# Two lanes of filler work, a count of three PSUM banks, and one weight transform issued beside the next

## The chip, the core and the metric

The kernel runs on one core of one Trainium2 chip. Its engines work side by side and each takes its instructions in the order in which they were issued: TensorE (PE in the profile, its weight loads PEld) multiplies matrices into PSUM; VectorE (DVE) and ScalarE (ACT) work on SBUF and PSUM; GpSimd (POOL) works on SBUF here; SyncE (SP) issues the DMAs. The metric is the device time of one execution in microseconds (us), and of several runs the median.

## The reference

Two transformer layers over x of 2 x 1024 x 256, each of the form x + attention(norm(x)) + feed-forward(norm(x)).

- Layer 0: linear attention with elu(q) + 1 and elu(k) + 1 (16 heads of 16), and a gated feed-forward of 256 -> 1024 -> 256 with weights rounded to -1, 0, 1 times a scale.
- Layer 1: softmax attention with rotary positions, and a gated feed-forward whose input and hidden vectors go through a Walsh-Hadamard transform (`fwht`) and sign vectors first:

```python
x = fwht(x * SU_ug) / SCALE
x_up = x @ W_up.T * (Wscale_ug[:INTER] * SCALE)
x_gate = x @ W_gate.T * (Wscale_ug[INTER:] * SCALE)
x = jax.nn.silu(x_gate) * x_up
x = fwht(x * SU_dp) / SCALE
x = x @ W_down.T * (Wscale_dp * SCALE)
```

The kernel moves these transforms from the activations to the weights, which are transformed once.

## The kernel before

**Phases.** Everything up to about 200 us (norms, layer 0's attention, most of its feed-forward, the first heads and the first maxima) is put in order by a planner: `Plan.emit` sorts recorded operations by estimated costs and by the table `LEADS`. From there on the order is written out by the loops at the end of the kernel, and it is this part that the change touches.

**Units.** Layer 1's attention is cut into 8 units (2 batches x 4 groups of 4 heads). The main loop runs over units 0 to 6; each has 32 steps, and each step issues one burst on PE: the scores of the next unit for their maxima (`scm`) and the scores of this unit for the exponentials (`sce`). DVE reduces `scm` to `peak` (1.22 us), ACT turns `sce` into `pr` (1.02 us), and `weigh` multiplies `pr` with the values into `po` every fourth step. A unit takes some 88 us in the profile: unit 2 from about 390 us, unit 4 from about 566 us. Unit 7 has no maxima to find and ends near 880 us.

**Filler.** Between bursts, `slot` lets PE do other work. Generators yield after each group of matmuls, with the group's cost by the program's constants; `fill` steps the generator at the head of the list `filler` until the slot's share is spent. The share is what is left of all such work (`left`) over the slots that are left (`to_fill`). The filler is, in order: layer 0's last feed-forward pieces, `norm1(2)`, the weight transforms `hadamards()`, `norm1(3)`, and the eight pieces of layer 1's feed-forward, `ffn1(0)` to `ffn1(7)`. `project(b, n)`, the output projection of a quarter of the attention, is put at place 1 of the list when its attention is ready (`queue_next`).

**Waits.** A generator that yields SOON has issued matmuls whose result has still to be drained from PSUM. The drains are issued at the next `go_on(SOON, ...)`, once in two steps, or at once if `fill` still owes more than `LEAD` = 0.85. If less is owed, `fill` breaks off. FIRST and SECOND are such points too.

**Heads.** In units 0, 2 and 4 `heads_of` makes the next heads. It stands in the list `urgent`, which `stage` steps in every second step: there `lay_out` transposes four tiles into one bank `pt`, `take_out` drains it with an ACT cast to `qk_hi` and a DVE subtraction to `ql`, and the next row's projection `pqkv` goes into another bank.

**Banks.** [...] Two tiles "pair" hold the scores (4 banks), `po` holds one, and three are general, tag "bank": every `pug` (gate and up of one 128-wide block of the hidden layer), `py` (down), `pw` (weight transforms), `pt` (transposes) and `pqkv` takes one of them. A tile's place comes free when its last reader has finished; a matmul into a new tile waits for that on PE, and everything behind it in PE's order with it.

**The transforms.** `hadamard_down` multiplies layer 1's down weights by a 128-wide transform on PE; `butterflies` does the remaining three stages over the eight blocks with additions on POOL and subtractions on DVE, and then multiplies by signs on ACT. It runs in the list `background`, one yield for each `go_on`, between `wd1` (tag "wC") and a second buffer `other` (tag "wB"). `hadamard_in` transforms the gate weights (tag "wA") and the up weights, whose result also has the tag "wB". `hadamards` therefore waits, between these two, until the background is empty:

```python
yield from hadamard_in("wgT1", "wA")
while background:
    yield 0.0, SECOND
yield from hadamard_in("wuT1", "wB")
```

## Time and profile before

| | before |
|---|---|
| median of 3 runs | 895.97 us |
| lowest, highest | 893.58, 896.11 us |
| the profiled execution | 894.11 us |
| its span in the profile | 892.3 us |
| mean granted clock of TensorE | 0.994 |

In the page, busy time is given for each engine with its share of the span; slices are fortieths of the span (22.3 us each) with one digit for the busy tenths; PEclk is the clock granted to TensorE, where 9 stands for 90% or more. In the timeline a row has the start, the length, the engine, the operation, what it writes and reads, and in brackets the idle time of the engine before it and what ended that. A count such as x4 is the number of records merged into the row; an f32 matmul leaves two records. All instructions carry the line 316 because a helper issues them, so tiles are told apart by name.

### The profile page before, as it was taken

The page shows a single profiled execution, that of the slowest core. Times are in us where ns is not written, and L with a number is a line of the kernel's source. Part 1 is how long each engine was busy: PE and PEld are TensorE (multiplying, and loading weights), DVE is VectorE, ACT ScalarE, POOL GpSimd, SP SyncE. Part 2 cuts the span into 40 slices and gives each one's busy share as a digit, 9 for nine tenths or more (in the row PEclk, how much of TensorE's full clock was granted, in tenths as well). Part 3 has the DMA queues.
Part 4 walks back from the last instruction along what each step waited for, and adds up shares of the span by engine and source line. Part 5 has one row for each costly group of instructions (what it writes and reads, how often), then busy time and mean ns, then how long its engine had stood idle before and what let it go on. Part 6 is the DMA issues. An engine that isn't in the chain of part 4 may idle for free.

```text
span 892.3 us, 14588 instructions
## 1 busy us (share of the span) xinstructions
PE 851.7 (95%) x6048; PEld 509.3 (57%) x6048; DVE 578.0 (65%) x950; ACT 445.0 (50%) x657; POOL 209.9 (24%) x283
## 2 busy tenths in 40 slices
PE   8999999989989979999999999998999999999997
PEld 5699866675456534555555555554555555555533
DVE  5887567887767776657766656667665656656211
ACT  6645464515655454535544444454454444444563
POOL 2656877513551220104400000143000000000000
PEclk9999999999999989999999999999999999999999
DMA  9200000000010110000000000000100000000001
GB/s 303 84 1 1 1 1 1 1 1 1 1 49 1 48 47 1 2 1 1 1 1 1 1 2 1 1 1 13 36 1 1 1 1 1 1 2 1 1 7 42
DMA packets 11313, 14.77 MB, mean 17 GB/s; under 512 B 1264, under 2 KB 8944, under 8 KB 11248
## 3 DMA queue, kind: packets, MB, share of 16 engines
q1 hardware_dynamic: 11248, 13.85, 4.7%
q8 instruction: 47, 0.77, 0.4%
q14 instruction: 18, 0.15, 0.1%
HBM read 11.75 MB, written 2.10 MB: 16 GB/s over the span
## 4 chain that ended last, share of the span: by engine, by line
PE 80%; DVE 12%; ACT 4%; issue 2%; DMA 1%; SPq 0%; POOL 0%; ACTq 0%; DVEq 0%
PE pug L316 18%; PE scm L316 15%; PE py L316 13%; PE po L316 12%; PE sce L316 8%; DVE peak L316 6%; PE pqkv L316 5%; PE pt L316 4%; PE pkv L316 1%; ACT pr L316 1%; PE sc L316 1%; PE pq L316 1%; PE pw L316 1%; DVE act L316 1%; DVE att L316 1%
## 5 line engine op out<-in xcount | busy, mean ns | idle before, releaser
L316 ACT ACTIVATE pr<-sce 128x1024 f32<-128x1024 f32 x256 | 260.3, 1023 | 270.9 <-PE sce L316 270.7
L316 DVE TENSOR_REDUCE peak<-scm 128x2 f32<-128x1024 f32 x224 | 274.1, 1224 | 177.6 <-PE scm L316 175.7
L316 PE MATMUL sce<-qk_hi 32*128 32x512 f32 x512 | 124.3, 497 | 3.0 <-ACT pr L316 2.1
L316 PE MATMUL po<-pr,va 128*17 128x512 f32 x1024 | 126.4, 603 | 0.0
L316 PE MATMUL scm<-qk_hi 32*128 32x512 f32 x448 | 112.2, 497 | 13.4 <-DVE peak L316 13.0
L316 PEld LDWEIGHTS scm<-qk_hi 32*128 32x128 f32 x448 | 41.7, 182 | 121.7 <-DVE peak L316 42.1
L316 PE MATMUL sce<-ql,qk_hi 32*128 32x512 f32 x512 | 98.3, 396 | 0.0
L316 PE MATMUL sce<-mx,ones_r 32*128 32x512 f32 x512 | 97.9, 394 | 0.1
L316 POOL CAST tops<-nm 128x16 fp32r<-128x16 f32 x16 | 3.4, 212 | 386.6 <-DVE nm L316 383.7
L316 PE MATMUL scm<-qk_hi,ql 32*128 32x512 f32 x448 | 89.8, 397 | 0.0
L316 PE MATMUL pug<-xnT,eff_wuT 128*128 128x256 f32 x256 | 71.4, 388 | 0.0
L316 PE MATMUL pug<-xnT,eff_wgT 128*128 128x256 f32 x256 | 70.5, 398 | 0.0
L316 PE MATMUL py<-wd,hid 128*128 128x256 f32 x256 | 65.6, 394 | 0.0
L316 DVE SCALAR_TENSOR_TENSOR act<-act,pug 128x256 f32<-128x256 f32 (+1 forms) x112 | 50.4, 451 | 19.8 <-ACT act L316 12.9
L316 PEld LDWEIGHTS po<-pr,va 128*17 128x17 f32 x1024 | 22.9, 97 | 63.3 <-issue 61.6
L316 PEld LDWEIGHTS py<-wd,hid 128*128 128x128 f32 x256 | 45.5, 190 | 19.6 <-issue 14.8
L316 POOL TENSOR_TENSOR hid<-act,hid 128x256 fp32r<-128x256 f32 (+1 forms) x48 | 44.6, 933 | 48.7 <-ACT hid L316 29.6
L316 PEld LDWEIGHTS pug<-xnT,eff_wgT 128*128 128x128 f32 x256 | 44.2, 189 | 20.0 <-issue 15.4
L316 PEld LDWEIGHTS sce<-qk_hi 32*128 32x128 f32 x512 | 46.2, 182 | 14.8 <-ACT pr L316 10.7
L316 PEld LDWEIGHTS pug<-xnT,eff_wuT 128*128 128x128 f32 x256 | 46.8, 190 | 12.7 <-issue 7.3
L316 PEld LDWEIGHTS sce<-mx,ones_r 32*128 32x128 f32 x512 | 47.1, 185 | 11.2 <-ACT mx L316 0.5
L316 PE MATMUL pqkv<-wqkvT,xnT 128*128 128x384 f32 x128 | 49.0, 502 | 1.5 <-DVE xnT L316 1.5
(145 smaller groups left out, 1310.4 us busy)
## 6 DMA issues: line engine op xcount, KB each, us to landing
out<-x SPq DMA_DIRECT2D x16, 128.0 KB, 1.7
x<-in_x SPq DMA_DIRECT2D x3, 512.0 KB, 9.5
both<-in_wuT SPq DMA_DIRECT2D x1, 1024.0 KB, 9.4
both<-in_wgT SPq DMA_DIRECT2D x1, 1024.0 KB, 11.1
wdT<-in_wdT SPq DMA_DIRECT2D x1, 1024.0 KB, 13.6
raw<-in_wdT SPq DMA_DIRECT2D x2, 512.0 KB, 3.6
raw<-in_wgT SPq DMA_DIRECT2D x2, 512.0 KB, 3.4
raw<-in_wuT SPq DMA_DIRECT2D x2, 512.0 KB, 3.8
```

What stands on the lines that cost most here:

```text
L316: return call(*map(real, args), **{k: real(v) for k, v in kw.items()})
```

## The change

1. **Two lanes.** A list `lanes` names generators that may run beside each other: the `ffn1` pieces but the second, and every `project`. Where `fill` would break off because the first generator in `filler` waits, and the first and the second are both lanes, it steps the second. The second `ffn1` piece becomes a lane when the butterflies are done. `go_on` now drains any of the first three generators in `filler` that wait, not only the first.
2. **Banks accounted for.** Once the written-out order has begun, `bank` counts the general banks in use, from the call to the new `shut(tile)`, which stands behind the last drain's issue. If three are in use, it first steps the generator with the oldest one until one is shut; `fill` does not start a new tile when there is no room. The count is one of the order of issue, not of time.
3. **Butterflies in place.** They work on `wd1` itself with small temporaries of the tag "hid1"; the second buffer goes, and with it the wait in `hadamards`. The first stage is done block by block (four instructions of 256 columns for each engine, where there were two of 512). `ffn1(0)` forces the background to an end before its down part.
4. **Hidden tiles in two rings.** "hid" with 8 places becomes "hid0" and "hid1" with 4 each: in layer 0 the halves of a piece, in layer 1 even and odd pieces.
5. **`project`** transposes its two halves one after the other, each drained before the next, where both stood in banks at once; it sends finished rows of the output when only its own part, or nothing, is missing.

```diff
     def bank(name):
-        return ps.tile([P, C], F32, tag="bank", name=name, bufs=3)
+        while ordered[0] and not has_room():
+            go(in_use[min(in_use)])
+        t = ps.tile([P, C], F32, tag="bank", name=name, bufs=3)
+        if ordered[0]:
+            in_use[taken[0]] = now[0]
+            t.root.number = taken[0]
+            taken[0] += 1
+        return t
+
+    def shut(t):
+        if ordered[0]:
+            del in_use[t.root.number]
...
     def take_out(cols, pt):
             scalar.copy(thk[:, :, cols], pt)
             vector.tensor_tensor(tl[:, :, cols], pt[:, 0:2, :], thk[:, 0:2, cols], ALU.subtract)
+            shut(pt)
...
     def butterflies(wd1, there):
-        other = const.tile([P, NB, D], F32, tag="wB", name="had_wd")
...
+        def two(n=2):
+            return [const.tile([P, 2, D], F32, tag="hid1", name="had_wd", bufs=4) for _ in range(n)]
...
+        for n in range(0, NB, 4):
             while n not in there:
                 yield 0.0, BOTH
+            t = two()
+            for i in range(2):
+                step(t[i][:, 0, :], t[i][:, 1, :], wd1[:, n + 2 * i, :], wd1[:, n + 2 * i + 1, :])
             yield 0.0, BOTH
+            step(wd1[:, n : n + 2, :], wd1[:, n + 2 : n + 4, :], *t)
             yield 0.0, BOTH
+        for n in range(0, 4, 2):
+            t = two()
+            step(*t, wd1[:, n : n + 2, :], wd1[:, n + 4 : n + 6, :])
             yield 0.0, BOTH
+            for i in range(2):
+                for e in range(n + 4 * i, n + 4 * i + 2):
+                    scalar.mul(wd1[:, e, :], t[i][:, e % 2, :], su_dp[:, e : e + 1])
+            yield 0.0, BOTH
+        lanes.append(filler[1])
 
     def hadamards():
         yield from hadamard_down()
         yield from hadamard_in("wgT1", "wA")
-        while background:
-            yield 0.0, SECOND
         yield from hadamard_in("wuT1", "wB")
...
-            lambda: None,
+            lambda: force(background) if cc == 0 else None,
...
+    def go(gen):
+        outer, now[0] = now[0], gen
+        x = next(gen, None)
+        now[0] = outer
+        if x is not None:
+            waits[gen] = x[1] if isinstance(x, tuple) else 0
+            new[gen] = cost_of(x) == 0.0
+            left[0] -= cost_of(x)
...
     def fill(us, queue, k=0):
         spent[k] = max(spent[k], -1.0) - us
+        def can(gen):
+            when = waits.get(gen, 0)
+            return not (
+                when in (FIRST, SECOND)
+                or (when == SOON and spent[k] > -LEAD)
+                or (new.get(gen, True) and when == 0 and not has_room())
+            )
+
         while spent[k] < 0 and queue:
-            when = waits.get(queue[0], 0)
-            if ordered[0] and (when in (FIRST, SECOND) or (when == SOON and spent[k] > -LEAD)):
+            if callable(queue[0]) or can(queue[0]):
+                step(queue, k)
+            elif len(queue) > 1 and queue[0] in lanes and queue[1] in lanes and can(queue[1]):
+                step(queue, k, 1)
+            else:
                 break
-            step(queue, k)
...
     def go_on(*when):
-        if filler and waits.get(filler[0], 0) in when:
-            step(filler)
+        for gen in filler[:3]:
+            if waits.get(gen, 0) in when:
+                spent[0] += go(gen) or 0.0
...
-    filler += [ffn1(cc) for cc in range(8)]
+    filler += [(lane if cc != 1 else lambda gen: gen)(ffn1(cc)) for cc in range(8)]
```

More of the change, by code (lines that the diff above doesn't have):

```diff
@@ L364, in tile_two_layers @@
     state = State()
+    ordered = [False]
     tensor, vector, scalar, gpsimd, sync = (
@@ L381, in pair, with has_room @@
         return ps.tile([P, 2, C], F32, tag="pair", name=name, bufs=2)
+    taken, in_use, now = [0], {}, [None]
+    def has_room():
+        return len(in_use) < 3
     def bank(name):
-        return ps.tile([P, C], F32, tag="bank", name=name, bufs=3)
+        while ordered[0] and not has_room():
[9 more added lines that the diff above has]
+            del in_use[t.root.number]
     po = ps.tile([P, C], F32, tag="po", name="po", bufs=1)
@@ L527, in ffn @@
             if e % 2 == 0:
-                two = const.tile([P, 2, F], F32, tag="hid", name="hid", bufs=8)
+                two = const.tile([P, 2, F], F32, tag=f"hid{cc % 2}", name="hid", bufs=4)
             h = two[:, e % 2, :]
             vector.scalar_tensor_tensor(h, pug[:, 1, :], scale(e), act, ALU.mult, ALU.mult)
+            shut(pug)
             hid.append(h)
@@ L543, in ffn @@
             vector.tensor_add(xc[c][:, t, :], py, xc[c][:, t, :])
+            shut(py)
             yield 0.0
@@ L739, in split @@
             act = acts.pop(0)
+            tag = f"hid{len(hid) // (NB // 2)}"
             if wide:
-                h = [const.tile([P, 2, F], F32R, tag="hid", name="hid", bufs=8) for _ in range(2)]
+                h = [const.tile([P, 2, F], F32R, tag=tag, name="hid", bufs=4) for _ in range(2)]
             else:
-                both = const.tile([P, 2, F], F32R, tag="hid", name="hid", bufs=8)
+                both = const.tile([P, 2, F], F32R, tag=tag, name="hid", bufs=4)
                 h = [both[:, s : s + 1, :] for s in range(2)]
@@ L777, in ffn0 @@
             acts.append(act)
+            if not wide:
+                shut(pug)
             yield 0.0
@@ L796, in ffn0 @@
             vector.tensor_add(xc[c][:, t, :], py[j], xc[c][:, t, :])
+            shut(py[j])
         yield 0.0
@@ L856, in take_out @@
             vector.tensor_tensor(tl[:, :, cols], pt[:, 0:2, :], thk[:, 0:2, cols], ALU.subtract)
+            shut(pt)
         def split_k(i):
@@ L904, in heads_of @@
             )
+            shut(pqkv)
             cos, sin = (
@@ L966, in hadamard_in @@
                 vector.scalar_tensor_tensor(eff[:, m, cols], pw[0], su_ug[:, m : m + 1], eff[:, m, cols], ALU.mult, op)
+            for t in pw:
+                shut(t)
             yield 0.0
@@ L984, in hadamard_down @@
                 )
+                shut(pw)
                 yield 0.0
-            there.append(n)
+            there.append(4 * n)
             if n == 0:
@@ L990, in butterflies, with step @@
     def butterflies(wd1, there):
-        other = const.tile([P, NB, D], F32, tag="wB", name="had_wd")
-        def step(src, dst, h, blocks):
-            s4, d4 = (
-                t[:, blocks, :].rearrange("p (a two b) n -> p a two b n", two=2, b=h) for t in (src, dst)
-            )
-            gpsimd.tensor_tensor(d4[:, :, 0], s4[:, :, 0], s4[:, :, 1], ALU.add)
-            vector.tensor_tensor(d4[:, :, 1], s4[:, :, 0], s4[:, :, 1], ALU.subtract)
-        for n in range(2):
+        def two(n=2):
+            return [const.tile([P, 2, D], F32, tag="hid1", name="had_wd", bufs=4) for _ in range(n)]
+        def step(total, difference, x, y):
+            gpsimd.tensor_tensor(total, x, y, ALU.add)
+            vector.tensor_tensor(difference, x, y, ALU.subtract)
+        for n in range(0, NB, 4):
             while n not in there:
                 yield 0.0, BOTH
-            blocks = slice(4 * n, 4 * n + 4)
-            step(wd1, other, 1, blocks)
+            t = two()
+            for i in range(2):
+                step(t[i][:, 0, :], t[i][:, 1, :], wd1[:, n + 2 * i, :], wd1[:, n + 2 * i + 1, :])
             yield 0.0, BOTH
-            step(other, wd1, 2, blocks)
+            step(wd1[:, n : n + 2, :], wd1[:, n + 2 : n + 4, :], *t)
             yield 0.0, BOTH
-        s2, d2 = (t.rearrange("p (two b) n -> p two b n", two=2) for t in (wd1, other))
-        for b in (slice(0, 2), slice(2, 4)):
-            gpsimd.tensor_tensor(d2[:, 0, b], s2[:, 0, b], s2[:, 1, b], ALU.add)
-            vector.tensor_tensor(d2[:, 1, b], s2[:, 0, b], s2[:, 1, b], ALU.subtract)
+        for n in range(0, 4, 2):
+            t = two()
+            step(*t, wd1[:, n : n + 2, :], wd1[:, n + 4 : n + 6, :])
             yield 0.0, BOTH
-        for e in range(NB):
-            scalar.mul(wd1[:, e, :], other[:, e, :], su_dp[:, e : e + 1])
-            if e == 3:
-                yield 0.0, BOTH
+            for i in range(2):
[3 more added lines that the diff above has]
+        lanes.append(filler[1])
     def hadamards():
@@ L1116, in put_peaks @@
         scalar.copy(mx[u, n], pt)
+        shut(pt)
         left[0] -= CT * P * TR / 2
@@ L1170, in normalise @@
         )
+        shut(pt)
         if g == NG - 1:
-            later(1, lambda: queue_next(project(b, n)))
+            later(1, lambda: queue_next(lane(project(b, n))))
         left[0] -= CT * P * TR
@@ L1179, in project @@
         aT = at.tile([P, 2, C], F32, tag="stage", name="aT", bufs=3)
-        pts = []
         for k in range(2):
-            pts.append(bank("pt"))
+            pt = bank("pt")
             for j in range(CT):
-                tensor.transpose(pts[k][:, j * P : (j + 1) * P], att[b, n][:, j, k * P : (k + 1) * P], ident)
-        yield 2 * CT * P * TR, SOON
-        scalar.copy(aT[:, 0, :], pts[0])
-        vector.tensor_copy(aT[:, 1, :], pts[1])
-        yield 0.0
-        parts_left[c] -= 1
-        last = parts_left[c] == 0
+                tensor.transpose(pt[:, j * P : (j + 1) * P], att[b, n][:, j, k * P : (k + 1) * P], ident)
+            yield CT * P * TR, SOON
+            (vector.tensor_copy if k else scalar.copy)(aT[:, k, :], pt)
+            shut(pt)
+            yield 0.0
+        to_send = list(range(CT))
         for j in range(CT):
@@ L1195, in project @@
             vector.tensor_add(xc[c][:, j, :], py, xc[c][:, j, :])
-            if last:
-                sync.dma_start(out=out_d[:, c * CT + j, :], in_=xc[c][:, j, :])
+            shut(py)
+            if j == CT - 1:
+                parts_left[c] -= 1
+            if parts_left[c] == (j < CT - 1):
+                for t in to_send:
+                    if t <= j:
+                        sync.dma_start(out=out_d[:, c * CT + t, :], in_=xc[c][:, t, :])
+                to_send = list(range(j + 1, CT))
             yield 0.0
@@ L1216, in tile_two_layers, with lane, step @@
     waits = {}
-    ordered = [False]
+    def lane(gen):
+        lanes.append(gen)
+        return gen
     def queue_next(gen):
         filler.insert(1, gen) if filler else filler.append(gen)
-    def step(queue, k=0):
-        if callable(queue[0]):
-            background.append(queue.pop(0)())
-            return
-        try:
-            x = next(queue[0])
-        except StopIteration:
-            queue.pop(0)
-            return
-        waits[queue[0]] = x[1] if isinstance(x, tuple) else 0
-        spent[k] += cost_of(x)
-        left[0] -= cost_of(x)
+    lanes = []
+    def go(gen):
[7 more added lines that the diff above has]
+        else:
+            for queue in (filler, urgent, background):
+                if gen in queue:
+                    queue.remove(gen)
+        return x and cost_of(x)
+    new = {}
+    def step(queue, k=0, at=0):
+        if callable(queue[at]):
+            background.append(queue.pop(at)())
+            return
+        spent[k] += go(queue[at]) or 0.0
     def fill(us, queue, k=0):
         spent[k] = max(spent[k], -1.0) - us
-        while spent[k] < 0 and queue:
-            when = waits.get(queue[0], 0)
-            if ordered[0] and (when in (FIRST, SECOND) or (when == SOON and spent[k] > -LEAD)):
+        def can(gen):
[5 more added lines that the diff above has]
+            )
+        while spent[k] < 0 and queue:
+            if callable(queue[0]) or can(queue[0]):
+                step(queue, k)
+            elif len(queue) > 1 and queue[0] in lanes and queue[1] in lanes and can(queue[1]):
+                step(queue, k, 1)
+            else:
                 break
-            step(queue, k)
         if not queue:
@@ L1254, in go_on @@
             if waits.get(gen, BOTH) in (*when, BOTH) and (FIRST in when or SECOND in when):
-                x = next(gen, None)
-                if x is None:
-                    background.remove(gen)
-                else:
-                    waits[gen] = x[1] if isinstance(x, tuple) and x[1] in (FIRST, SECOND) else BOTH
+                if go(gen) is not None:
+                    waits[gen] = waits[gen] if waits[gen] in (FIRST, SECOND) else BOTH
     def stage():
@@ L1272, in force @@
             if queue is background:
-                run(queue.pop(0))
+                go(queue[0])
             else:
```

## The prediction

> **What bounds the kernel now.** First the page's busy times and slices.

> ```profile
> PE 851.7 (95%) x6048; PEld 509.3 (57%) x6048; DVE 578.0 (65%) x950; ACT 445.0 (50%) x657; POOL 209.9 (24%) x283
> PE   8999999989989979999999999998999999999997
> PEclk9999999999999989999999999999999999999999
> ```

> TensorE is the bound; the change removes no matmul. So it can only close holes in PE (892.3 - 851.7 = 40.6 us) or raise the granted clock, which dips in one slice (the digit 8). Five-us windows locate the holes: about 10 us before 200 (planned order, not the aim of the change), 7 in 200-300, 6 in 300-350, 9 in 350-850 (600-625 has 2.9 of it), 7 after 850, filler being exhausted. Then the waits, PE only, whole span:

> ```profile
> PE scm L316 <- DVE peak L316: 13.0, 25, 1.1
> PE py L316 <- ACT aT L316: 2.5, 3, 1.6
> PE pqkv L316 <- DVE xnT L316: 1.5, 1, 1.5
> PE pug L316 <- DVE act L316: 1.4, 1, 1.4
> PE pw L316 <- ACT eff_wgT L316: 1.2, 1, 1.2
> ```

> (total, times, longest.) The first row is what PE does when a slot brings no filler: the next score burst reaches its "pair" tile before the last maximum is out. The pqkv and pug rows are the three general banks running out. Windows, columns as in the page (PE, PEld, DVE, ACT, POOL, clock, DMA):

> ```profile
> 245.00:250.00 5.00, 2.57 (x22) 1.87 (x22) 3.43 (x9) 2.40 (x5) 3.50 (x7) 1.00 0.33 108
> 325.00:330.00 5.00, 3.65 (x26) 1.83 (x22) 3.17 (x4) 2.75 (x5) 0.00 (x0) 0.69 0.00 0
> 330.00:335.00 5.00, 4.51 (x26) 1.72 (x24) 2.45 (x2) 4.52 (x9) 0.00 (x0) 0.50 0.00 0
> 335.00:340.00 5.00, 5.00 (x27) 1.55 (x20) 1.23 (x1) 1.02 (x1) 0.00 (x0) 0.79 0.02 3
> ```

> **Part 1, down's transform beside the last weights'.** In the PE timeline the last wgT transform matmul is at 317.34 and the first of wuT at 338.15; between them stand only scores and weighings, because `hadamards` yields SECOND while the butterflies run. Idle in 315-345 is 30 - 24.5 = 5.5 us. The clock rows above cost 3.65 x 0.31 + 4.51 x 0.50 + 5 x 0.21 = 4.4 us. Without the wait, wuT's four matmul pairs (about 1 us each) follow at once, and ffn1(0), which began at 343.5, at about 326.

> Does the clock come back? [...] I take the row: 5.5 + 4.4 = 9.9.

> What is late next is DVE: it is 5.00 busy in 320-325 already. Per pair of steps it will have two maxima at 1.22, some 1.3 transform drains at 1.40 and two butterfly halves at 0.68, 5.6 us, beside about 5.3 us of PE. I leave 1.5 us for that: **gain 8.4**, ends 4 (DVE takes over) and 10. The new butterflies are eight instructions on each of DVE and POOL in place of six: DVE 4 x 0.41 + 4 x 0.68 = 4.4 for 4.1, POOL 4 x 0.73 + 4 x 1.26 = 8.0 for 7.6, under PE's work. wuT's raw DMAs left at 312.5-314.5 and take 3.8 us to land, so 318.4 at the latest, for a use near 319-322: free, 1 us if late. The `force(background)` before ffn1(0)'s down finds nothing left: nine butterfly steps, one per burst pair from 308.7, end near 331; ffn1(0) needs 32 matmuls of 0.48, 15.5 us of filler, before it gets there. It also follows that ffn1(1) joins the lanes at about 331.

> **Part 2, two lanes: the gain.** `fill` breaks off when its generator waits with SOON and under LEAD (0.85) is owed; the second lane then supplies matmuls. That is 15 of the 25 waits on `peak`, in 345-830, 0.45 each, 6.7 us:

> ```profile
> 461.42 0.70 PE L316 MATMUL pug<-xnT,eff_wuT 128*128 128x256 f32 x2
> 462.57 0.49 PE L316 MATMUL scm<-qk_hi 32*128 32x512 f32 x2 [0.45 <-DVE peak L316]
> ```

> One matmul, then a hole. The lane fills most: **gain 5**, ends 2 and 6.7. The hole of projection (0,1) near 615-623 (1.6 + 0.9 + 0.4) may be partly filled, but its lane also takes a bank; I put 0, ends -2 and +2.

> **Part 3, two lanes: the price.** There are still three banks. Lane A (first in the queue) nearly always holds one: half a `pug`, a whole one whose drain is only issued at the next go_on(SOON), or a `py` for eight matmuls. Lane B advances only in the leftovers, so once opened it stays open over many slots. That leaves one bank. In units 2 and 4 `heads_of` runs beside this, and its stage needs two in a row: `pt` is transposed, and `pqkv` follows at once. Today:

> ```profile
> 407.07 0.33 PE L316 MATMUL pt<-ident,rot 128*128 128x128 f32 x1
> 407.47 1.51 PE L316 MATMUL pqkv<-wqkvT,xnT 128*128 128x384 f32 x4
> 408.16 0.58 ACT L316 CAST qk_hi<-pt 128x512 fp32r<-128x512 f32 x1
> 408.78 0.42 DVE L316 TENSOR_TENSOR ql<-pt,qk_hi 128x256 fp32r<-128x256 f32 x1 [0.60 <-ACT qk_hi L316]
> ```

> `pqkv` starts 0.4 us after `pt`, in a third bank. With A and B open it must wait for `ql` to end, 409.20, plus 0.15 for the signal (between the end of `act` at 245.94 and the matmul at 246.09), less 407.47: **1.9 us**. The cast stands behind the exponential on ACT, so this repeats: the six stages of unit 2 with both tiles, and the six of unit 4, all give 1.72 to 1.74 before the signal. The bookkeeping doesn't prevent it: `has_room` counts program order, and there `pt` is already shut. Queued behind the waiting matmul on PE are filler and the next bursts, so ACT and DVE starve too; nothing hides it. The same happens where `pqkv` follows the maxima's `pt` (mx ends 398.12, pqkv 396.81: 1.5) or `normalise`'s (1.4), once each per unit.

> The trace of before has a fourth user of the banks once, norm1(2)'s `pt` in unit 0:

> ```profile
> 246.09 0.71 PE L316 MATMUL pug<-xs,t_wuT 128*128 128x256 f32 x4 [1.43 <-DVE act L316]
> 250.17 1.53 PE L316 MATMUL pqkv<-wqkvT,xnT 128*128 128x384 f32 x4 [1.51 <-DVE xnT L316]
> ```

> How often are both lanes open? By hand through unit 2: a heads stage costs 2 x 0.64 + 0.32 = 1.6 by the program's constants, about the slot's whole share (some 1.5), so filler comes mainly in every fourth step, three or four matmuls of 0.43. Starting with both half full, which the 65 us of slots between 331 and 396 make likely, A and B stay open over both first stages and four of the six double ones, until both reach SOON together: 1.5 + 1.4 + 4 x 1.9 = 10.5 per unit, **21 us** in units 2 and 4. Ends: two double stages per unit (7.6), and every one with the two later `pt` pairs (11.4 + 2.9 + 2.9 = 17.2 per unit, 34).

> Elsewhere A re-opens while `normalise` or `pqkv` is still draining, which a third bank used to cover: I put **2 us**, ends 0 and 8 (four such tiles in each of six units, a third of them at 1.4).

> [...] But 245-250 has PE at 2.57 of 5 us from two bank waits and a clock of 1.00. I take the row: 0.

> **Parts at nothing.** Splitting `hid` into `hid0`/`hid1` keeps every buffer's reuse distance at eight; only the planner's in-order rule relaxes, so the first 200 us may reshuffle: 0, ends -1 and +1. `project`'s transposes one at a time need one bank fewer and add one slot's wait; its pieces of output leave on SP earlier or at the same point, 1.7 us to land as before. The background's cost now comes off `left`: 1.7 us of 264, nothing.

> **Sum.** -8.4 - 5 + 21 + 2 = +9.6 us. The profiled execution took 894.1 (span 892.3 + 1.8), the median of before is 896.0: 903.7 by the first, 905.6 by the second. I allow for stalls that overlap the holes they replace and say **903**.

> **Rivals.**
> 1. *Lane B is mostly shut during heads* (chance 0.22, faster). For it: filler is thin there, and go_on now drains both lanes. Against: B gets the least of it, and a partial tile has no drain. Two double stages per unit: 894.1 - 13.4 + 7.6 = 888. It decides below about seven stalls in the twelve double stages (13.4 / 1.9).
> 2. *DVE takes over in 318-340* (0.12, slower): part 1 yields 4 and the clock still dips: 894.1 - 4 - 5 + 23 = 908.
> 3. *Every stage stalls* (0.10, slower), because projections inserted at place 1 leave a half-full third piece behind them in unit 4: 894.1 - 13.4 + 34 + 2 = 917.
> 4. *Gain and price meet* (0.12): some eight stalls; within 0.3% (2.7 us, about what a measurement of this kernel can tell from no change) of 896.

> The forecast has 0.44, all slower; its own range is 899 to 909. Slower 0.44 + 0.12 + 0.10 = 0.66, same 0.12, faster 0.22. The range 888 to 917 leaves out the outer parts of rivals 1 and 3.

> **What would show it.** Part 1: wuT's `pw` right after wgT's, clock 1.00 through 320-345, DVE near full there. Part 2: fewer than 8 waits of scm on `peak` after 345. Part 3: a new row, PE pqkv waiting for DVE `ql`, some 8 times at 1.5 to 2 us, inside units 2 and 4, and PE down from 51.5 of 52 us in 396-448 to about 52 of 62. If that row is missing or has under 2 us, the forecast is wrong on its largest term; if the clock still falls near 330, on its second.

## The result and the profile after

| | before | after |
|---|---|---|
| median | 896.04 us (4 runs) | 906.28 us (4 runs) |
| lowest, highest | 893.58, 896.25 | 902.98, 907.32 |
| the profiled execution, its span | 894.11, 892.3 us | 905.55, 903.8 us |
| mean granted clock of TensorE | 0.994 | 0.992 |

The changed kernel takes 1.0114 times as long, with a 95% interval of 1.0082 to 1.0147: about 10 us slower. The page's busy times and slices after:

```profile
PE 853.1 (94%) x6048; PEld 509.7 (56%) x6048; DVE 576.1 (64%) x952; ACT 445.0 (49%) x657; POOL 210.9 (23%) x285
PE   8999999999889989998999999999899999999997
PEclk9999999999999999999999999999999999999999
```

PE has the same 6048 matmuls, and its busy time is 1.4 us more; idle time grew from 40.6 to 50.7 us. The 8 in the clock row is gone, but the mean clock is not higher: four short dips (3.4 us each at a clock of 0.50, from 248.4, 371.3, 429.3 and 613.7 us) are now spread over several slices, which still round to 9. PE's waits over the whole span (total, times, longest):

```profile
PE pqkv L316 <- DVE ql L316: 6.5, 4, 1.6
PE scm L316 <- DVE peak L316: 5.4, 10, 1.1
PE pt L316 <- DVE att L316: 3.3, 5, 1.2
PE pqkv L316 <- DVE att L316: 2.4, 2, 1.2
PE pqkv L316 <- ACT mx L316: 2.4, 2, 1.2
PE pug L316 <- DVE xnT L316: 1.8, 1, 1.8
```

The holes before the scores fell from 13.0 to 5.4 us; new rows stand above and below. They are the banks: `pqkv` waits for `ql`, for `att` and for `mx`, the three drains that the prediction had named. Of the four waits for `ql`, three lie in unit 2 and one in unit 4. In PE's timeline of unit 2:

```profile
418.77 0.33 PE L316 MATMUL pt<-ident,rot 128*128 128x128 f32 x1
420.95 1.56 PE L316 MATMUL pqkv<-wqkvT,xnT 128*128 128x384 f32 x4 [1.62 <-DVE ql L316]
428.27 1.91 PE L316 MATMUL pqkv<-wqkvT,xnT 128*128 128x384 f32 x4 [1.62 <-DVE ql L316]
```

From `pt` to `pqkv` it is 2.18 us where it was 0.40, so 1.8 us late. The second such wait is followed by `pqkv` at 1.91 us instead of 1.5: the granted clock is 0.50 from 429.3 to 432.7.

The next table takes as landmarks ten of the sixteen casts of the maxima's tiles (`mx`), which both traces have, and says how much later the changed kernel reaches each:

| landmark before at | 203 | 256 | 302 | 353 | 398 | 484 | 571 | 662 | 748 | 833 us |
|---|---|---|---|---|---|---|---|---|---|---|
| later by, us | 2.1 | 3.3 | 3.1 | 1.9 | 2.7 | 13.8 | 11.9 | 16.2 | 12.7 | 12.2 |

Unit 2 loses 11 us, unit 4 some 4 to 6; the rows 571, 748 and 833 stand lower than those before them, so 0.5 to 3.5 us are won back in units 3, 5 and 6; 2 us are lost before the written-out order has begun; and the transform part, between 302 and 398, wins hardly anything.

### The profile page after: what moved, and what is told of

Same layout as the page of the kernel before. It is cut to its first block, busy times and chain, and to the rows that moved or that the text cites. A ratio compares the mean times of both kernels' runs of the same rounds, so it can differ in the third digit from the quotient of the medians.

```text
span 903.8 us, 14600 instructions
## 1 busy us (share of the span) xinstructions
PE 853.1 (94%) x6048; PEld 509.7 (56%) x6048; DVE 576.1 (64%) x952; ACT 445.0 (49%) x657; POOL 210.9 (23%) x285
## 4 chain that ended last, share of the span: by engine, by line
PE 79%; DVE 12%; ACT 5%; issue 2%; DMA 1%; POOL 0%; SPq 0%; ACTq 0%; DVEq 0%
PE pug L316 18%; PE scm L316 15%; PE py L316 13%; PE po L316 12%; PE sce L316 7%; DVE peak L316 5%; PE pqkv L316 5%; PE pt L316 3%; ACT pr L316 2%; PE pkv L316 2%; PE pq L316 1%; PE sc L316 1%; DVE act L316 1%; DVE att L316 1%; ACT xn L316 1%
## 5 line engine op out<-in xcount | busy, mean ns | idle before, releaser
L316 ACT ACTIVATE pr<-sce 128x1024 f32<-128x1024 f32 x256 | 260.5, 1024 | 289.0 <-PE sce L316 288.8
L316 DVE TENSOR_REDUCE peak<-scm 128x2 f32<-128x1024 f32 x224 | 274.1, 1224 | 185.7 <-PE scm L316 183.8
L316 PE MATMUL sce<-qk_hi 32*128 32x512 f32 x512 | 123.1, 498 | 2.1 <-ACT pr L316 1.8
L316 PE MATMUL po<-pr,va 128*17 128x512 f32 x1024 | 124.8, 596 | 0.0
L316 PE MATMUL scm<-qk_hi 32*128 32x512 f32 x448 | 112.4, 498 | 6.3 <-DVE peak L316 5.4
L316 PEld LDWEIGHTS scm<-qk_hi 32*128 32x128 f32 x448 | 41.6, 183 | 113.8 <-DVE peak L316 38.8
L316 PE MATMUL sce<-ql,qk_hi 32*128 32x512 f32 x512 | 97.4, 395 | 0.0
L316 PE MATMUL sce<-mx,ones_r 32*128 32x512 f32 x512 | 97.3, 394 | 0.1
L316 POOL CAST tops<-nm 128x16 fp32r<-128x16 f32 x16 | 3.4, 211 | 375.0 <-DVE nm L316 372.4
L316 PE MATMUL scm<-qk_hi,ql 32*128 32x512 f32 x448 | 89.5, 395 | 0.0
L316 PE MATMUL pug<-xnT,eff_wgT 128*128 128x256 f32 x256 | 71.7, 401 | 3.1 <-DVE xnT L316 1.8
L316 PE MATMUL pug<-xnT,eff_wuT 128*128 128x256 f32 x256 | 73.7, 395 | 0.0
L316 PE MATMUL py<-wd,hid 128*128 128x256 f32 x256 | 67.6, 396 | 2.3 <-DVE att L316 1.2
L316 DVE SCALAR_TENSOR_TENSOR act<-act,pug 128x256 f32<-128x256 f32 (+1 forms) x112 | 50.5, 451 | 20.1 <-ACT act L316 15.3
L316 PE MATMUL pqkv<-wqkvT,xnT 128*128 128x384 f32 x128 | 50.3, 513 | 12.5 <-DVE ql L316 6.5
L316 PEld LDWEIGHTS pug<-xnT,eff_wgT 128*128 128x128 f32 x256 | 45.2, 191 | 23.4 <-issue 14.3
L316 PEld LDWEIGHTS po<-pr,va 128*17 128x17 f32 x1024 | 22.8, 96 | 62.6 <-issue 60.9
L316 PEld LDWEIGHTS py<-wd,hid 128*128 128x128 f32 x256 | 44.9, 189 | 22.8 <-issue 17.0
L316 POOL TENSOR_TENSOR hid<-act,hid 128x256 fp32r<-128x256 f32 (+1 forms) x48 | 44.1, 921 | 49.2 <-ACT hid L316 30.1
L316 PEld LDWEIGHTS pug<-xnT,eff_wuT 128*128 128x128 f32 x256 | 47.1, 194 | 13.7 <-issue 8.4
L316 PEld LDWEIGHTS sce<-mx,ones_r 32*128 32x128 f32 x512 | 46.6, 185 | 11.2 <-ACT mx L316 0.5
L316 PEld LDWEIGHTS sce<-qk_hi 32*128 32x128 f32 x512 | 45.8, 182 | 11.4 <-ACT pr L316 8.3
## 6 DMA issues: line engine op xcount, KB each, us to landing
both<-in_wgT SPq DMA_DIRECT2D x1, 1024.0 KB, 10.3
```

Of the source, the lines that this page charges most:

```text
L316: return call(*map(real, args), **{k: real(v) for k, v in kw.items()})
```

## The experiments

Where a wait is named by L318, two lines had been added above the helper. A clock dip is, in what follows, a stretch of 3.4 us at a granted clock of 0.50, as the changed kernel has from 248.4 to 251.8 us; I put its cost to PE at half of that, 1.7 us, an estimate.

**rings_only: the hidden tiles' two rings alone, on the kernel before.**

```diff
-                two = const.tile([P, 2, F], F32, tag="hid", name="hid", bufs=8)
+                two = const.tile([P, 2, F], F32, tag=f"hid{cc % 2}", name="hid", bufs=4)
...
+            tag = f"hid{len(hid) // (NB // 2)}"
...
-                h = [const.tile([P, 2, F], F32R, tag="hid", name="hid", bufs=8) for _ in range(2)]
+                h = [const.tile([P, 2, F], F32R, tag=tag, name="hid", bufs=4) for _ in range(2)]
```

> The kernel before with only the hidden tiles in two rings of four. Theory P (the two rings relax the planner's in-order rule, and the new order of the first 200 us is the worse one): the first cast of the maxima stands at 205.2 us instead of 203.1, and the time is 1 to 3 us above before. Rival Q (the 2 us lost before 205 us come from something else in the change, or from chance): no difference, within 0.5 us.

896.96 us, ratio 1.0021 (1.0004 to 1.0038): 0.4 to 3.4 us slower, 1.9 by the ratio. The first cast of the maxima stands 1.8 us later. PE's order is that of the kernel before up to 117 us and from there on the changed kernel's, to past 200 us. So the two rings do change the plan, for the worse by a little. The trace can't give the size: it has a clock dip at 120 us (four records of `pug` from `t_wgT` take 1.05 us there, 0.63 in the changed kernel) that by the estimate alone costs 1.7, while the changed kernel is 2.1 us late at 203 without one.

**one_order: the changed kernel, with one common order for the two rings**, so that PE's order is that of before up to 203 us, and up to 264 us if the score matmuls are left aside.

```diff
...
-        root = ring.latest = Root(
+        kind = tag.rstrip("01") if tag in ("hid0", "hid1") else tag
+        root = self.last[kind] = Root(
...
-            ring.latest,
+            self.last.get(kind),
```

> The changed kernel with one common in-order rule for the two rings, so that the planned part is that of before, instruction by instruction. Theory P: 2 to 3 us less than the changed kernel, so 7 to 9 us above before, and the first cast of the maxima at 203.1. Rival Q: as the changed kernel, 10 us above before. Units 2 and 4 keep their losses of about 11 and 6 us in both.

901.91 us, ratio 1.0065 (1.0048 to 1.0081). The first cast is back within 0.2 us of before, and 4.4 us of the loss are gone, more than the 2 to 3 expected; units 2 and 4 lose what they lost. Theory P holds in kind; its size is 1.9 us alone and 4.4 us here, and the table below shows that part of the difference is clock.

**one_order_no_lane: the same without the second lane.**

```diff
-            elif len(queue) > 1 and queue[0] in lanes and queue[1] in lanes and can(queue[1]):
+            elif False and len(queue) > 1 and queue[0] in lanes and queue[1] in lanes and can(queue[1]):
```

> As one_order, but fill never steps the second lane; the transform beside wuT's, the count of banks and the split projection stay. Theory B (the second lane's open bank is the price): the waits of pqkv for ql, att and mx vanish, units 2 and 4 take what they took before, and the time falls below before by what the transform part is worth: by the prediction 8 us (888), by the trace of the changed kernel (2 us gained from 302 to 352 us, and a bank wait of 1.8 and a clock dip after that belong to the lane) 3 to 6 us. Rival R (the count of banks or the transform part costs the time): still 3 us or more above before.

884.26 us, ratio 0.9874 (0.9853 to 0.9895). The waits of `pqkv` for `ql`, `att` and `mx` are gone, and the holes before the scores are back:

```profile
PE scm L318 <- DVE peak L318: 11.0, 22, 1.1
```

The lanes cost 901.9 - 884.3 = 17.6 us, and without them the rest of the change makes the kernel 11.6 us faster. Rival R has fallen; the gain is more than the 3 to 8 us expected. Part of it is clock: four of the six executions have a granted clock of 1.000, which no execution of the kernel before has (0.987 to 0.996).

**one_order_no_heads: the second lane only where no heads are made.**

```diff
-            elif len(queue) > 1 and queue[0] in lanes and queue[1] in lanes and can(queue[1]):
+            elif len(queue) > 1 and not urgent and queue[0] in lanes and queue[1] in lanes and can(queue[1]):
...
                 force(background)
+                for gen in filler[1:3]:
+                    while gen in in_use.values():
+                        go(gen)
             urgent.append(heads_of(*((0, 1), (1, 0), (1, 1))[u // 2]))
```

> As one_order, but the second lane is stepped only while no heads are made, and its open tile is finished before a heads unit begins. Theory B: the price of units 2 and 4 (11 + 6 us) goes and the gain of the lanes in the other units (1.4 to 1.9 us each in units 3, 5 and 6) stays: 5 to 9 us below before, 2 to 4 below one_order_no_lane. Rival R: like one_order. Rival S (the gain of units 3, 5 and 6 was only filler left over from units 2 and 4 that had to be done at some time, no gain): equal to one_order_no_lane within 1 us.

886.60 us, ratio 0.9881 (0.9863 to 0.9900). The price in units 2 and 4 is gone (15.3 us less than one_order), but the lanes gain nothing elsewhere: 2.3 us above one_order_no_lane, intervals overlapping. The waits say why; PE in this kernel:

```profile
PE scm L318 <- DVE peak L318: 6.8, 13, 1.1
PE pug L318 <- DVE att L318: 3.1, 3, 1.2
PE pug L318 <- DVE xnT L318: 1.8, 1, 1.8
```

Without lanes the first row is 11.0 us and the other two don't exist. So 4.2 us of holes were filled, and 4.9 us of new bank waits made: a new `pug` stands behind `normalise`'s and the norm's transposes. Of expectation B only half was right. S was right that nothing is gained, but the 2.3 us are more than its 1 us, and the reason is another than it gave.

**held_24: no lanes, but one bank taken away in units 2 and 4** (an unused tile; one transpose into it and one small read are added).

```diff
...
-        return len(in_use) < 3
+        return len(in_use) < 3 - held[0]
...
+        if u in (2, 4):
+            h = ps.tile([P, C], F32, tag="bank", name="held", bufs=3)
+            tensor.transpose(h[:, 0:P], ident, ident)
+            held[0] = 1
         for i in range(0, STEPS, 2):
...
+        if u in (2, 4):
+            scrap = small.tile([P, CT], F32, tag="scrap", name="scrap")
+            vector.tensor_copy(scrap, h[:, 0:CT])
+            held[0] = 0
```

> one_order_no_lane (884.3 us) with one of the three general banks held by an unused tile through units 2 and 4, one transpose into it and one small read of it added, and no second lane. Theory B (what costs in the heads units is the missing bank, nothing else of the lanes): every heads stage with pt and pqkv now waits 1.6 us for ql, six in each unit, and four more tiles in each wait about 1.2 us for mx or att: 2 x (6 x 1.6 + 4 x 1.2) = 29 us above one_order_no_lane, 20 at least; the rows pqkv waiting for ql, mx and att come back in units 2 and 4. Rival V (the lanes cost by the changed order of the matmuls or by clock dips, and the bank waits merely replace other waits): less than 8 us above one_order_no_lane.

917.49 us, ratio 1.0250 (1.0228 to 1.0273): 33 us above one_order_no_lane. PE's waits in the whole span:

```profile
PE pqkv L318 <- DVE ql L318: 11.0, 7, 1.6
PE pqkv L318 <- DVE att L318: 2.4, 2, 1.2
```

The missing bank alone, with no lane and no piece out of order, brings back the changed kernel's rows and more than its loss; rival V has fallen. It was seven stalls on `ql`, not twelve; other bank waits in unit 4 (`pt` for `va` 1.7, `py` for `ql` 1.4 and more) and the clock dips in those two units, some 6 to 7 us (the granted clock is 0.94 from 575 to 665), come on top.

**held_35: the same in units 3 and 5**, `u in (3, 5)`.

> The same with the bank held through units 3 and 5, where no heads are made (unit 5 has the projections). Theory B: a bank less costs little there, since one filler tile and one passing tile need two: 0 to 4 us above one_order_no_lane, from new tiles that open while normalise's or the maxima's transposes drain. If it is 4 us or more, that is what took the lanes' gain away in one_order_no_heads.

890.80 us, ratio 0.9943 (0.9929 to 0.9958): 6.5 us above one_order_no_lane, so above the 4 that I had set as the mark. By landmarks the loss comes in two jumps of 3.0 us, each one new wait of `pug` for `att` (1.2 us) and a clock dip (1.7 us by the estimate, at 533 and 711 us; the execution's granted clock is 0.990):

```profile
PE pug L318 <- DVE att L318: 2.4, 2, 1.2
```

A bank is worth something there too. The same row, with 3.1 us, was among the new waits of one_order_no_heads, so this fits what ate the lanes' gain there.

**old_project: no lanes, and `project` as before** (both transposes in two banks, then both drains; rows are sent as before, too).

```diff
-            pt = bank("pt")
+            pts.append(bank("pt"))
...
-            yield CT * P * TR, SOON
-            (vector.tensor_copy if k else scalar.copy)(aT[:, k, :], pt)
-            shut(pt)
-            yield 0.0
+        yield 2 * CT * P * TR, SOON
+        scalar.copy(aT[:, 0, :], pts[0])
+        vector.tensor_copy(aT[:, 1, :], pts[1])
+        for t in pts:
+            shut(t)
+        yield 0.0
...
```

> one_order_no_lane with project as before: both transposes in two banks at once, then both drains. The trace of one_order_no_lane gains 2.5 us on before between 612 and 660 us, where the first two projections run. Theory W (that gain is the split projection's): 2 to 3 us above one_order_no_lane, near 887. Rival X (it is the filler that the transform part brought forward, so that less is left for this unit): equal to one_order_no_lane within 1 us.

893.34 us, ratio 0.9976 (0.9966 to 0.9986): 9 us above one_order_no_lane, three times what W expected. PE's timeline at the second projection:

```profile
625.25 1.09 PE L318 MATMUL pt<-ident,att 128*128 128x128 f32 x8
629.05 3.65 PE L318 MATMUL py<-woT,aT 128*128 128x256 f32 x8 [1.60 <-ACT aT L318]
```

The windows there (stretch and its length, busy time of PE, PEld, DVE, ACT and POOL with their instructions, granted clock, share of the DMA engines, GB/s):

```profile
627.00:631.00 4.00, 2.40 (x11) 1.62 (x8) 1.82 (x2) 1.50 (x2) 0.00 (x0) 0.78 0.00 0
631.00:635.00 4.00, 4.00 (x21) 2.61 (x21) 2.01 (x4) 1.02 (x1) 0.00 (x0) 0.80 0.10 33
```

Eight records of `py` take 3.65 us there, and 1.99 from 633.5 on, after the dip. Both projections of unit 4 have such a hole (1.77 and 1.60) with a dip behind it, 6.8 us together; in one_order_no_lane one hole of 0.96 is left and no dip.

**split_project: the kernel before with only `project` changed**, the reverse of the diff above without `shut`.

> The kernel before with only the change of project: one transposed half at a time, each drained before the next, and the new sending of rows. Theory W (the split is what separates old_project, 893.3, from one_order_no_lane, 884.3): the waits of py for aT, 2.8 us in before and 5.3 in old_project, fall to about 1.3, and the hole at 614 to 623 us shrinks: 2 to 5 us below before without a clock dip spared, up to 9 with. Rival X (the 9 us are clock dips alone): equal to before within 1 us, the waits on aT as in before or replaced by others as long.

895.42 us, ratio 0.9998 (0.9981 to 1.0014): nothing. Alone, the split doesn't even fill the hole (`py` for `aT` 2.9 us, before 2.5), probably because the slot still owes more than LEAD and goes on at once; X came true here in its number, and W there in kind. The 9 us belong to the meeting of both: no sum of single parts gives them.

**lead_04 and lead_00: no lanes, and `fill` drains and goes on earlier.**

```diff
-    LEAD = 0.85
+    LEAD = 0.4
```

> one_order_no_lane with LEAD 0.4 instead of 0.85: fill breaks off only when less than 0.4 is owed, so it drains and goes on with its own next tile where a second lane would have helped, without a second open tile. If the holes before the scores (22 waits of scm for peak, 11.0 us) are what a second lane should fill, half of them go this way: 2 to 4 us below one_order_no_lane. Rival Y (the drains then stand in ACT's and DVE's order ahead of the exponentials and maxima and delay them as much): within 1 us, or above.

879.33 us, ratio 0.9825 (0.9807 to 0.9843), 4.9 below one_order_no_lane, more than the 2 to 4 expected.

```profile
PE scm L318 <- DVE peak L318: 1.9, 5, 0.8
```

The holes that the second lane was to fill are closed by a smaller number in the first lane's own rule, with one open tile. With 0.0:

> one_order_no_lane with LEAD 0.0: fill never breaks off at SOON, it always drains and goes on. lead_04 (879.3) took the waits of scm for peak from 11.0 to 1.9 us, so little is left to win: 0 to 2 us below lead_04. Rival Y (drains issued too early stand ahead of maxima and exponentials): above lead_04 by 1 us or more.

876.86 us, ratio 0.9795 (0.9765 to 0.9826): some 2.5 us less, though the intervals overlap. Rival Y has fallen in both.

**before_lead_04: the kernel before with LEAD 0.4 and nothing else.**

> The kernel before with LEAD 0.4 and nothing else. Theory Z (the holes before the scores are closed by draining earlier, without a second lane and whatever else is changed): as from one_order_no_lane to lead_04, 3 to 6 us below before. Rival Y: within 1 us of before.

886.06 us, ratio 0.9900 (0.9873 to 0.9927): 9.5 us faster, more than Z expected. The first row of PE's waits, 13.0 us before, is now:

```profile
PE scm L316 <- DVE peak L316: 4.4, 7, 1.1
```

The extra is not luck with the clock dips: the six executions have a mean clock of 0.988 to 0.994, no better than before (0.987 to 0.996).

**old_project_again: the program of old_project, executed once more.**

> The program of old_project once more, one look. In its first profile the clock fell to half three times, at 250, 605 and 629 us, each time for 3.4 us and right after a hole of 1.4 to 1.8 us in PE. Theory D (whether such a hole halves the clock is decided by its place in a window that runs free of the program): the holes stand where they stood, and the dips are at other holes, or fewer or more. Rival E (the program decides): dips at the same three places.

893.46 us. Dips at 206, 247, 605 and 629 us: the two behind the projections came again, the one near 250 came 3.5 us earlier, and one is new. This does not decide between D and E. In both traces the clock changes only at the edges of steps of 3.41 us (the last section has the figures), and these steps lay almost alike in the two executions: they begin 1.17 us after the first instruction in one and 1.08 us in the other, so D, too, gives dips at nearly the same places. The dip that moved came one step earlier. Which hole of 1.4 to 1.8 us is followed by half clock stays open.

**Waits and clock apart.** Each execution's mean granted clock is on record. An estimate of what half clock cost it is its span times one minus that clock, as if PE had been the bound throughout; the rest of the time is what it would have taken at full clock. The clock is on record to 0.001, which is 0.9 us of a span, so only means are used. Means over the executions of each program, in us:

| program | executions | mean time | half clock | rest |
|---|---|---|---|---|
| before, three series | 19, 33, 19 | 895.8, 896.1, 895.2 | 7.4, 8.1, 7.0 | 888.3, 888.1, 888.2 |
| after | 4 | 905.7 | 7.2 | 898.5 |
| rings_only | 14 | 897.7 | 7.9 | 889.8 |
| one_order | 6 | 902.5 | 5.9 | 896.6 |
| one_order_no_lane | 6 | 885.4 | 1.2 | 884.2 |
| one_order_no_heads | 5 | 886.8 | 1.9 | 884.9 |
| held_24 | 4 | 917.9 | 8.7 | 909.2 |
| held_35 | 20 | 891.2 | 4.3 | 886.9 |
| old_project | 12 | 893.2 | 5.1 | 888.2 |
| split_project | 14 | 895.0 | 7.0 | 888.1 |
| lead_04 | 5 | 879.3 | 2.5 | 876.9 |
| lead_00 | 6 | 876.9 | 3.5 | 873.4 |
| before_lead_04 | 6 | 886.1 | 8.3 | 877.9 |

The rest of the kernel before came out alike three times, so differences of 1 us in that column mean something. The changed kernel's 10 us are all in the rest; half clock costs it as much as before, at other places. The rings cost 1.5 us of rest alone and 1.9 in company. The lanes cost 12.4 us of rest and 4.7 of clock. Of the split projection's value 4.0 us are rest, as much as the waits of `py` for `aT` differ (5.3 us against 1.3), and 3.9 are clock. The held bank costs 25.0 us of rest in units 2 and 4 and 2.7 in units 3 and 5. LEAD 0.4 saves 7.3 us of rest in one_order_no_lane and 10.3 in the kernel before.

## Why the prediction came out, step by step

It gave 903 us, 888 to 917, slower with 0.66; measured 906.3. The decisive step held. Several terms around it were off, and that their sum came out so near is in part luck.

**Part 3, the price in units 2 and 4: right, and shown.** Three banks, a second open tile, `pqkv` behind the drain of `pt`: the delay of one is 1.8 us where 1.9 was worked out. held_24 shows that the bank alone does it, one_order_no_heads that 15.3 us belong to those units; 21 was put. Some 11.7 of them are waits and 3.9 clock. The count was too high and the cost of each too low: four stalls on `ql` instead of eight, but some of the stalls were followed by clock dips (0.50 from 429.3 and from 613.7 us).

**The clock during stalls: wrong.** I took 0 because the window 245-250 of before had bank waits and full clock. The changed kernel has dips at 248, 371, 429 and 613 us, each with a bank wait before it (1.43, 1.77, 1.62 and 1.63 us), by the estimate 1.7 us apiece. The first follows the very wait that the zero rested on, `pug` for `act` with 1.43 us, which the changed kernel meets 2.1 us later. The window of before had a clock of 1.00; the matmul that took 0.71 us there, and the window, are now:

```profile
248.21 1.00 PE L316 MATMUL pug<-xs,t_wuT 128*128 128x256 f32 x4 [1.43 <-DVE act L316]
245.00:250.00 5.00, 3.57 (x27) 2.59 (x25) 2.88 (x6) 1.93 (x4) 2.59 (x4) 0.84 0.36 110
```

PE's timeline at the second of them:

```profile
371.18 1.93 PE L316 MATMUL pug<-xnT,eff_wgT 128*128 128x256 f32 x4 [1.77 <-DVE xnT L316]
```

And the window there, with a clock of 0.66:

```profile
370.00:375.00 5.00, 3.82 (x12) 2.66 (x16) 1.85 (x4) 0.67 (x2) 0.00 (x0) 0.66 0.00 0
```

One window that stayed at 1.00 was too little evidence for a zero. Here waits of 1.43 to 1.77 us stood before half clock; what decides it was not shown.

**Part 1, gain 8.4: the clock came back, the idle time didn't go.** The window of the same stretch, after:

```profile
315.00:345.00 30.00, 25.39 (x158) 11.23 (x157) 22.38 (x36) 17.67 (x28) 6.74 (x7) 1.00 0.11 36
```

Clock 1.00, so the 4.4 us were there to win, but idle is still 4.6 of the 5.5 us; I had left 1.5. That filler is what brings the clock back, as those 4.4 us supposed, no run shows: in the trace of before the clock is 0.50 from 326.9 to 337.1 us and 1.00 again before the first `pw` of wuT at 338.15; what the runs show is 1.00 in this stretch with the transforms side by side. The text named DVE as next. What the trace shows is something smaller: each transform's second half waits 1.2 us for ACT's drain (`pw` for `eff_wgT`, once more for `eff_wuT`), and `scm` for `peak` 1.1. In time, the transform part is worth 2.5 us with old_project and 11.6 with the split projection. By the table the 2.5 us are all clock (3.0 by the means) and none of them rest: what idle time it saved was lost again in the projections, where `py` waits 5.3 us for `aT` instead of 2.8.

**Part 2, gain 5: filled, but not gained.** The waits of scm on `peak` after 345 us fell from 15 to 3 (6.7 to 1.1 us), as put. Their place was taken by the bank waits that the term "elsewhere, 2 us" stood for. That term was too small: one_order_no_heads has 4.9 us of such waits, and held_35 shows what a bank is worth in two of these units, 6.5 us. Its upper end was also worked out wrongly, as a third of 24 tiles at 1.4 us is 11.2 us and not 8.

**Parts at nothing: two of them weren't.** The hidden rings were put at 0 with ends of 1: 1.9 us alone, 4.4 in company, of which 1.5 and 1.9 are waits. The split projection was put at nothing and is worth 9 us or none, by what stands around it. A smaller slip is in the reading of the holes: between 350 and 850 us PE is idle for 10.6 us, not 9.

So the sum +9.6 came near the measured +10.2 with errors that cancelled. It holds -4.4 us of clock and +14.0 of waits and idle time; the table has -0.2 and +10.1. The clock won back near 330 us was lost again behind the stalls, and the stalls themselves were fewer than put. The chain of kernels splits the 10.4 us between its ends into transform and projection -11.6, lanes +17.6, rings +4.4; these add up by construction, and another order of steps could share them out differently. Rival 1 (B mostly shut) had the right count of stalls on `ql` and still the wrong sign: it kept the whole gain of 13.4 us and counted no other waits (`att`, `mx`), no rings and no dips against it.

## What to carry to other kernels

Count buffers in time, not only in order of issue: a tile that is "shut" in the program still holds its bank until its drain has run, and a second half-finished accumulation takes a bank away from whoever needs two in a row (here `pqkv` waited four times for `ql`, 6.5 us). Before adding a second source of work to fill holes, see whether the first one breaks off by a threshold of its own; here that one number was worth more than the lanes, and the version with it (no lanes, LEAD 0.0, 876.9 us) beats both kernels. When a kernel's plan is tuned against one set of buffer tags, a change of tags alone is a change of order: keep the order rule and the tags apart.

## What the runs showed of the hardware

In the changed kernel four holes in PE (1.43, 1.77, 1.62 and 1.63 us, up to 248.2, 371.2, 428.3 and 613.0 us) were each followed by 3.41 us at a granted clock of 0.50, by the estimate 1.7 us beside the hole itself. In the kernel before, a hole of 1.59 us up to 617.9 was not. Of programs whose filler on PE has one order up to 264 us, before had no such dip in that stretch, old_project one, from 250.3 us, and old_project_again two, from 205.9 and 246.8 us.

Busy time alone doesn't decide: in old_project the step from 243.5 to 246.9 has 2.0 us, and the next has a clock of 1.00. What else counts was not found, and differences of 2 us between single profiles of this kernel should not be read as structure.
